# A four-layer graph network on one core: the last group's layer 3 in two parts with a plain product and early statistics, in place of gate products by TensorE and a held TensorE order in the head

## The chip, the cores and the metric

The kernel runs on one core of one Trainium2 chip. The metric is the time of one execution on the device in microseconds (us); the median of several executions is what is compared. The engines are TensorE (PE in the profile; its weight loads are PEld), VectorE (DVE), ScalarE (ACT), GpSimd (POOL) and SyncE (SP), which here only issues transfers. All data is float32.

## The reference, cut to what matters

The input `x` is 128 graphs of 128 nodes by 256 features; `adj` is one 128x128 matrix. Four layers follow one another, each of the form x = x + f(relu(layernorm(x))):

```
# layer 0: gated message passing
in_gate = h @ gate_weight + bias_gate            # one number per node; three such gates
msg_in  = (adj @ h + edge_bias) * sigmoid(in_gate)
msg_out = (adj' @ h + out_edge_bias) * sigmoid(out_gate)
x = x + relu(msg_in + msg_out + h * sigmoid(lp_gate))
# layer 1: causal attention, one head, width 256, adj added to the scores
# layer 2: three graph convolutions, widths 256 -> 512 -> 1024 -> 256, weighting adj*adj
# layer 3:
agg = A_hat @ h                                   # A_hat: normalized adjacency
h1  = relu(batchnorm(agg @ W1.T + b1, g1, be1))   # 256 -> 512
out = batchnorm(h1 @ W2.T + b2, g2, be2)          # 512 -> 256
x   = x + out
```

The two batchnorms of layer 3 take mean and variance per feature over all 128 x 128 rows. Nothing behind the first batchnorm can start before the last graph's product with W1 is known, and nothing behind the second before the last product with W2.

## The kernel before, in words

Graphs are taken in 32 groups of four (G = 4, `NG` = 32, `LAST` = 31); with columns as nodes a group is T = 512 wide.

**First pass** (lines 115 to 851). Layers 0, 1, 2 and the first half of layer 3 run group by group. Each layer is a Python generator (`layer0`, `layer1`, `layer2`, `layer3`) that yields between steps. A string says which generator advances next: `FILL` (line 818) for the head, where group 0 runs in two halves of two graphs (`a`, `c` for layer 0, `b`, `d` for layer 1), `A` is layer 0 of group 1, `p` is `prepare` (weights turned and combined) and `w` stands for 12 idle turns; `TURN` (line 805) for each group; `FINAL` (line 808) for the last one. In `TURN` and `FINAL`, `C` is layer 2 of the group, `D` layer 3 of the group before, `d` layer 3 of this group. The strings set priorities; a scheduler then lays out each engine's queue, and may bring forward what it holds ready. In the head `in_turn` (line 86) holds TensorE's instructions to the order of the string. Instructions given through `keep_in_program_order` keep theirs.

**Products by seven.** `seven` (line 454) computes a product of two 2x2 block matrices with seven half-size products instead of eight: operands are sums of blocks (`sums`, line 406, four VectorE operations; `seven_of`, line 231, for weights), and results are put together through `kept` copies on ScalarE (line 461) and sums on VectorE in `put`. Its accumulators are x, y and z (`pz_x`, `pz_y`, `pz_z` in layer 3), x being used five times.

**Norm** (line 357). For each graph bn_stats and bn_aggr on VectorE give mean and variance; 1/sqrt is a `pow` on GpSimd; ScalarE applies scale, shift and ReLU (line 378). For whole groups the four small steps are on GpSimd (lines 369 to 372); for halves eps and shift are on VectorE (lines 219 and 375) and only `pow` on GpSimd (line 221).

**Layer 0** (line 489). Groups 0 and 1 (`g < 2`): `turn` transposes `h` on TensorE into `h0T`, and three-column products with `gwT` give the gates (line 504). Other groups: twelve scalar_tensor_tensor on VectorE with accumulator (line 513) against `gw`, the gate weights broadcast to all partitions. Then a sigmoid (line 521), and the mixing matrix `cmb` from `ain`, `aout` and `ident` scaled by the gates (lines 530 to 537), with the `eb` copies behind (line 539).

**Layer 3** (line 767). Norm, product with `ahT` into `gT` (`mixed`, `pg`), sums, then `seven` with the turned W1. In `put` ScalarE copies or VectorE sums a quarter into `z`; when both halves of a column pair are in, bn_stats takes 512 columns per feature chunk into `stats1` (line 789) and `z` goes to DRAM, except for the last group, which stays.

**Crossing.** Groups 0 to 29 are aggregated early (`most1`); after the loop `last1` takes groups 30 and 31, TensorE turns `ident` 60 times (`awake(60)`), and `bn_affine` (line 853) joins both into a scale and a shift per feature.

**Second pass** (lines 878 to 1002). Group 31 first, then 0 to 30 (`ORDER`): ReLU with scale and shift on ScalarE (line 939), the product with W2 by `seven` (`po_x`, `po_y`, `po_z`), results `O` kept in SBUF, statistics through `TOLD`/`tell`: for each half of the features one bn_stats of 512 columns, told one step later (line 921). **End:** `last2` takes the last group of the order, `bn_affine` again, then for each group scale and shift on ScalarE (line 1017), transposes on TensorE, the sum with `x` on VectorE (line 1030) and the store. Loads of `x` for this (`x3i`) start during the second pass and go on during the stores.

**Loads in the head.** `adj` on ScalarE's queue, the gate weights once as three rows on GpSimd's queue (for `gwT`), and everything else on SP in the order of the code, `gw` after w3. A dummy sigmoid on one column (line 189) loads the sigmoid table at the start.

Of the kernel before, what the change touches and what calls it, by code (L numbers as in the profile page):

```python
# [22 lines left out]
def kernel(  # L23
# [60 lines left out]
    behind = {}  # L84

    def in_turn(at, engines):

        for i in nc.cur_bb.bb.instructions[at:]:
            if i.engine in engines:
                if i.engine in behind:  # L90
                    tc.add_manual_dep(
                        i, behind[i.engine],
                        mybir.DependencyInfo(
                            mybir.DependencyClass.NoSync, mybir.DependencyReason.DATA
                        ),
                        reason="in_turn",
                    )
                behind[i.engine] = i.name

# [18 lines left out]
    nc.scalar.dma_start(adj_sb, adj)  # L118
# [31 lines left out]
    stats1 = weights.tile([P, FC, NG, 6], FP, name="stats1")  # L150
    stats2 = const.tile([P, DC, NG, 6], FP, name="stats2")

    nc.gpsimd.memset(nhalf, -0.5)
    nc.gpsimd.memset(gb, 0.0)
    w = passA.enter_context(tc.tile_pool(name="work", bufs=2))
# [22 lines left out]

    gwr = bw2t[:3, 0, :]
    gwT = weights.tile([P, DC, 3], FP, name="gwT")  # L180
    for i, v in enumerate((gate_weight, out_gate_weight, loop_gate)):
        nc.gpsimd.dma_start(
            gwr[i : i + 1, :], bass.AP(tensor=v.tensor, offset=v.offset, ap=[[D, 1], [1, D]])
        )
    nc.sync.dma_start(gb[:, 0:1], bias_gate)
    nc.sync.dma_start(gb[:, 1:2], out_bias_gate)

    table = const.tile([P, 1], FP, name="table")
    nc.scalar.activation(table, nhalf[:, 0:1], AF.Sigmoid)

# [13 lines left out]
    for i, v in enumerate((gate_weight, out_gate_weight, loop_gate)):  # L204
        nc.sync.dma_start(
            gw[:, i, :], bass.AP(tensor=v.tensor, offset=v.offset, ap=[[0, P], [1, D]])
        )
# [55 lines left out]
    pw = bank([P, DC, 3], "pgw")  # L263
    for c in range(DC):
        nc.tensor.transpose(pw[:, c, :], gwr[:, c * P : (c + 1) * P], ident[:3, :3])
    nc.vector.tensor_copy(gwT, pw)
# [8 lines left out]
    def prepare():  # L275
# [57 lines left out]
        yield  # L333
        SETS["b"] = seven_of(bw1T, "bw1T")
# [22 lines left out]
    def norm(g, layer, bs=ALL):  # L357
# [8 lines left out]
        rs = small.tile([P, n], FP, tag="rs", name=f"rs{tail}")  # L366
        sh = small.tile([P, n], FP, tag="sh", name=f"sh{tail}")
        if n == G:
            nc.gpsimd.tensor_scalar(rs, mv[:, :, 1], LN_EPS, None, ALU.add)  # L369
            nc.gpsimd.tensor_tensor(rs, rs, nhalf[:, :n], ALU.pow)  # L370
            nc.gpsimd.tensor_scalar(sh, mv[:, :, 0], -1.0, None, ALU.mult)
            nc.gpsimd.tensor_tensor(sh, sh, rs, ALU.mult)  # L372
        else:
            inv_sqrt(rs, mv[:, :, 1], LN_EPS)
            nc.vector.scalar_tensor_tensor(sh, mv[:, :, 0], -1.0, rs, ALU.mult, ALU.mult)
# [10 lines left out]

    def turn(dst, h, bs, name):

        for c in range(DC):
            pt = bank([P, len(bs), P], f"{name}_{c}")  # L390
            for k, b in enumerate(bs):
                nc.tensor.transpose(pt[:, k, :], h[:, b, c * P : (c + 1) * P], ident)
            evict = nc.vector.tensor_copy if c else nc.scalar.copy
            evict(columns(dst, c, bs), pt.rearrange("p b n -> p (b n)"))
# [94 lines left out]
    def layer0(g, bs=ALL):  # L489
# [5 lines left out]
        gate_bias = gb[:, None, :].to_broadcast([P, n, 3])  # L495
        if g < 2:

            hT = tile_of(g, bs, [P, DC, T], "dT", f"h0T_{g}", 2)
            turn(hT, h, bs, f"ph_{tail}")
            yield  # L500
            pl = bank([P, n, 3], f"pl_{tail}")
            for k, b in enumerate(bs):
                for c in range(DC):
                    nc.tensor.matmul(
                        pl[:, k, :], hT[:, c, b * P : (b + 1) * P], gwT[:, c, :],
                        start=(c == 0), stop=(c == DC - 1),
                    )
            nc.vector.tensor_tensor(gl, pl, gate_bias, ALU.add)
        else:
            gs = w.tile([P, D], FP, tag="gs", name=f"gs_{tail}", bufs=1)  # L510
            for k, b in enumerate(bs):
                for i in range(3):
                    nc.vector.scalar_tensor_tensor(  # L513
                        gs, h[:, b, :], 1.0, gw[:, i, :], ALU.mult, ALU.mult,
                        accum_out=gl[:, k, i : i + 1],
                    )
                if k == n // 2 - 1:
                    yield
            nc.vector.tensor_tensor(gl, gl, gate_bias, ALU.add)
# [18 lines left out]
        for k, b in enumerate(bs):  # L538
            nc.scalar.activation(bias[:, b, :], eb, AF.Copy, scale=gt[:, k, 0:1])
# [227 lines left out]
    def layer3(g):  # L767
# [11 lines left out]
        def put(ij, pb, other):  # L779
            i, j = ij  # L780
            dst = z[j][:, :, i * T // 2 : (i + 1) * T // 2]
            if other is None:
                nc.scalar.copy(dst, pb)
            else:
                nc.vector.tensor_tensor(dst, pb, other, ALU.add)
# [285 lines left out]
```

## Time and profile before

Time before: median 2590.16 us of 5 executions, 2589.49 to 2592.59.

| | |
|---|---|
| profiled execution, time | 2592.59 us |
| its span in the trace | 2590.6 us |
| mean granted TensorE clock | 0.993 |
| first layer-2 product of group 0 starts | 72.68 us |
| period of a steady group in the first pass | 70.8 us |
| last layer-3 product of the first pass ends | 2315.67 us |
| first product of the second pass starts | 2322.05 us |
| period of a group in the second pass | 6.04 us |
| last product of the second pass starts | 2517.14 us |
| first scaling for the output starts | 2522.47 us |
| last store issued from | 2579.50 us |

The page of the profile gives busy times and the span in 40 slices. The timeline lists instructions in order of time: start, length, engine, line, operation, output and inputs, shape, count, and in brackets the idle time of the engine before it and what ended that. A float32 matmul shows as two records; a transpose as one. The busy time by windows gives, for a stretch, its length, the busy time of PE, PEld, DVE, ACT and POOL with the number of instructions, the granted clock, the share of the DMA engines and GB/s.

### The profile page before, as it was taken

The numbers are of one execution on the slowest core, as the hardware profiler recorded it, in microseconds if no ns is written. First come the engines' busy times: TensorE is split into PE (matmuls) and PEld (weight loads), VectorE is DVE, ScalarE is ACT, GpSimd is POOL, SyncE is SP. The second block draws the span as 40 slices with busy tenths as digits, with TensorE's granted clock in tenths as the row PEclk, the third lists the DMA queues.
The fourth block names the chain that finished last, engine by engine and source line by source line (L and its number), as shares of the span: only waits on it lengthen the run. The fifth ranks groups of instructions, "written<-read, shape, count | busy, mean of one in ns | idle before, by whom it ended". The sixth has DMA issues, their size and how long they took to land.

```text
span 2590.6 us, 40769 instructions
## 1 busy us (share of the span) xinstructions
PE 2539.6 (98%) x15331; PEld 2295.0 (89%) x15331; DVE 1907.1 (74%) x4788; ACT 1288.6 (50%) x2576; POOL 288.1 (11%) x566
## 2 busy tenths in 40 slices
PE   7999999999999999999999999999999999999995
PEld 5999999999999999999999999999999999888875
DVE  6777777777777777777777777777777776558876
ACT  4554445444444554444444445544454444337766
POOL 1111011111111111011111110111111111000001
PEclk9999999999999999999999999999999999999998
DMA  3000000000000000000000000000000000035559
GB/s 134 15 34 33 33 33 25 25 33 34 33 26 25 33 33 33 33 33 24 26 33 34 33 25 26 33 33 33 34 33 17 34 25 25 25 123 192 176 185 386
DMA packets 49656, 143.07 MB, mean 55 GB/s; under 512 B 4258, under 2 KB 23220, under 8 KB 45492
## 3 DMA queue, kind: packets, MB, share of 16 engines
q1 hardware_dynamic: 42740, 116.81, 12.3%
q0 software_dynamic: 6576, 23.60, 2.6%
q8 instruction: 121, 1.98, 0.3%
q14 instruction: 75, 0.61, 0.1%
q10 hardware_dynamic: 144, 0.07, 0.0%
HBM read 73.48 MB, written 66.98 MB: 54 GB/s over the span
## 4 chain that ended last, share of the span: by engine, by line
PE 94%; DVE 1%; DMA 1%; ACT 1%; POOL 0%; issue 0%; SPq 0%; DVEq 0%; POOLq 0%
PE p_x L446 17%; PE p_x L429 9%; PE p_z L446 8%; PE pmu L401 4%; PE p_z L429 4%; PE pz_x L446 4%; PE p_y L446 4%; PE po_x L951 4%; PE pu_x L429 4%; PE pg L401 2%; PE ps L630 2%; PE pm L555 2%; PE p_y L429 2%; PE pqv_x L587 2%; PE py L660 2%; PE pr L760 2%
## 5 line engine op out<-in xcount | busy, mean ns | idle before, releaser
L378 ACT ACTIVATE h<-x,sh,rs 128x256 f32<-128x256 f32 x512 | 268.8, 589 | 356.8 <-POOL sh L372 346.1
L446 PE MATMUL p_x<-uT,w 128*128 128x256 f32 x1024 | 242.2, 379 | 0.0
L732 ACT ACTIVATE h2T<-h2T 128x512 f32<-128x512 f32 x192 | 120.6, 628 | 229.8 <-DVE h2T L731 229.8
L446 PEld LDWEIGHTS p_x<-uT,w 128*128 128x128 f32 x1024 | 189.7, 190 | 23.2
L363 DVE BATCH_NORM_STATS2 st<-x 128x6 f32<-128x256 f32 x512 | 191.0, 414 | 2.2
L369 POOL TENSOR_SCALAR rs<-mv 128x4 f32<-128x4 f32 x125 | 29.8, 239 | 1351.6 <-ACT h2T L732 1061.0
L513 DVE SCALAR_TENSOR_TENSOR gs<-h,gw 128x256 f32<-128x256 f32 x360 | 150.3, 418 | 27.6 <-ACT h L378 22.4
L461 ACT COPY p_t<-p_x 128x512 f32<-128x512 f32 (+1 forms) x192 | 96.6, 503 | 109.7 <-PE p_x L446 102.8
L370 POOL TENSOR_TENSOR rs<-rs,nhalf 128x4 f32<-128x4 f32 x125 | 145.0, 1160 | 0.0
L401 PEld LDWEIGHTS pmu<-a2T,u 128*128 128x128 f32 x1024 | 119.3, 192 | 14.8 <-issue 14.8
L429 PEld LDWEIGHTS p_x<-w,h2T 128*128 128x128 f32 x1024 | 124.3, 192 | 3.3
L685 ACT ACTIVATE u<-u 128x512 f32<-128x512 f32 x93 | 58.6, 631 | 133.7 <-DVE u L684 133.7
L429 PE MATMUL p_x<-w,h2T 128*128 128x128 f32 x1024 | 124.6, 275 | 0.0
L446 PE MATMUL p_x<-us,w_s 128*128 128x256 f32 x512 | 121.2, 379 | 0.0
L446 PE MATMUL p_x<-uT,w_s 128*128 128x256 f32 x512 | 121.1, 379 | 0.0
L446 PE MATMUL p_y<-uT,w 128*128 128x256 f32 x512 | 121.0, 379 | 0.0
L446 PE MATMUL p_z<-us,w_s 128*128 128x256 f32 x512 | 121.0, 379 | 0.0
L446 PE MATMUL p_z<-us,w 128*128 128x256 f32 x512 | 121.0, 379 | 0.0
L401 PE MATMUL pmu<-a2T,u 128*128 128x128 f32 x1024 | 119.5, 275 | 0.0
L761 DVE TENSOR_TENSOR x<-pr,x 128x512 f32<-128x512 f32 x64 | 43.7, 682 | 90.4 <-PE pr L760 90.4
L446 PEld LDWEIGHTS p_z<-us,w_s 128*128 128x128 f32 x512 | 97.3, 190 | 13.2
L446 PEld LDWEIGHTS p_z<-us,w 128*128 128x128 f32 x512 | 97.3, 190 | 13.2
(317 smaller groups left out, 6174.1 us busy)
## 6 DMA issues: line engine op xcount, KB each, us to landing
z<-zo SPq DMA_DIRECT2D x62, 512.0 KB, 2.6
zi<-z SPq DMA_DIRECT2D x31, 1024.0 KB, 4.8
x<-x POOLq DMA_DIRECT2D x32, 512.0 KB, 3.4
x<-in_x_dram SPq DMA_DIRECT2D x31, 512.0 KB, 4.0
out_dram<-x3i SPq DMA_DIRECT2D x30, 512.0 KB, 12.8
x3i<-x SPq DMA_DIRECT2D x19, 512.0 KB, 5.2
x3i<-x POOLq DMA_DIRECT2D x13, 512.0 KB, 10.1
w<-in_L_gnn_W_dram SPq DMA_DIRECT2D x1, 2048.0 KB
```

The source lines that it names most:

```text
L363: nc.vector.bn_stats(st[:, k, :], xt[:, b, :])
L370: nc.gpsimd.tensor_tensor(rs, rs, nhalf[:, :n], ALU.pow)
L378: nc.scalar.activation(h[:, b, :], xt[:, b, :], AF.Relu, bias=sh[:, k : k + 1], scale=rs[:, k : k + 1])
L401: nc.tensor.matmul(pm[:, k, :], src[:, b, c * P : (c + 1) * P], aT, start=True, stop=True)
L429: nc.tensor.matmul(pb[:, rr, :], a_r[r][:, c, rr * P : (rr + 1) * P], b_r[r][:, c, :wide], start=(first and rr == 0 and c == 0), stop=(c = ...
L446: nc.tensor.matmul(pb[:, jj, :], b_r[r][:, c, at : at + P], a_r[r][:, c, :], start=(first and jj == 0 and c == 0), stop=(c == nk - 1), ski ...
L461: nc.scalar.copy(t, pb)
L513: nc.vector.scalar_tensor_tensor(gs, h[:, b, :], 1.0, gw[:, i, :], ALU.mult, ALU.mult, accum_out=gl[:, k, i : i + 1],)
L555: nc.tensor.matmul(pm[:, r, :], cmbT[:, b, :], h[:, b, :], start=True, stop=True)
L685: nc.scalar.activation(dst, dst, AF.Relu)
L732: nc.scalar.activation(dst, dst, AF.Relu)
L951: nc.tensor.matmul(pb, BW2R[r][:, c, :], a_r[r][:, c, :], start=(first and c == 0), stop=(c == FC // 2 - 1), skip_group_check=True,)
```

## The change: what it does

In the head: the gates of groups 0 and 1 are computed as in all other groups, on VectorE; `turn`, `gwT` and its loads and turns, the dummy sigmoid and `in_turn` go; `FILL` is another string; half norms take the four GpSimd steps of whole norms; `adj` is loaded by SP ahead of `x`, and `gw` and the two gate biases by ScalarE's queue at the start; the `eb` copy of each graph is given ahead of its `ain` copy. In layer 3: groups 30 and 31 give their statistics by halves of 256 columns, from PSUM and ahead of the copy where ScalarE copies; group 31 takes its norm and its product with `ahT` in two halves and multiplies with W1 plainly, by quarters (i, j), without `sums` and `seven`; a copy `bw1T_12` keeps the block of W1 that `seven_of` overwrites. `FINAL` is another string, `awake(60)` becomes `awake(44)`. `bn_affine` has its steps in another order and two fewer after `pow`. In the second pass the last group's statistics are taken by halves in the same way.

```diff
-    nc.scalar.dma_start(adj_sb, adj)
+    nc.sync.dma_start(adj_sb, adj)
...
+    stats1 = weights.tile([P, FC, NG + 2, 6], FP, name="stats1")
+    stats2 = const.tile([P, DC, NG + 1, 6], FP, name="stats2")
+    bw1T_12 = weights.tile([P, F1 // 2], FP, name="bw1T_12")
...
+    for i, v in enumerate((gate_weight, out_gate_weight, loop_gate)):
+        nc.scalar.dma_start(
+            gw[:, i, :], bass.AP(tensor=v.tensor, offset=v.offset, ap=[[0, P], [1, D]])
+        )
+    nc.scalar.dma_start(gb[:, 0:1], bias_gate)
+    nc.scalar.dma_start(gb[:, 1:2], out_bias_gate)
...
-    table = const.tile([P, 1], FP, name="table")
-    nc.scalar.activation(table, nhalf[:, 0:1], AF.Sigmoid)
...
         yield
+        nc.scalar.copy(bw1T_12, bw1T[:, 0, F1 // 2 :])
         SETS["b"] = seven_of(bw1T, "bw1T")
...
+        nc.gpsimd.tensor_scalar(rs, mv[:, :, 1], LN_EPS, None, ALU.add)
+        nc.gpsimd.tensor_tensor(rs, rs, nhalf[:, :n], ALU.pow)
         sh = small.tile([P, n], FP, tag="sh", name=f"sh{tail}")
-        if n == G:
...
-            inv_sqrt(rs, mv[:, :, 1], LN_EPS)
-            nc.vector.scalar_tensor_tensor(sh, mv[:, :, 0], -1.0, rs, ALU.mult, ALU.mult)
+        nc.gpsimd.tensor_scalar(sh, mv[:, :, 0], -1.0, None, ALU.mult)
+        nc.gpsimd.tensor_tensor(sh, sh, rs, ALU.mult)
...
-        if g < 2:
-
-            hT = tile_of(g, bs, [P, DC, T], "dT", f"h0T_{g}", 2)
-            turn(hT, h, bs, f"ph_{tail}")
...
         for k, b in enumerate(bs):
+            nc.scalar.activation(bias[:, b, :], eb, AF.Copy, scale=gt[:, k, 0:1])
             nc.scalar.activation(cmb[:, b, :], ain, AF.Copy, scale=gt[:, k, 0:1])
...
-        for k, b in enumerate(bs):
-            nc.scalar.activation(bias[:, b, :], eb, AF.Copy, scale=gt[:, k, 0:1])
...
+        parts = [ALL] if g < LAST else HALVES
+        for bs in parts:
+            h = norm(g, 3, bs)
+            yield
+        gT = tile_of(g, parts[0], [P, DC, T], "dT", f"gT_{g}", 2)
+        for i, bs in enumerate(parts):
+            mixed(gT, h, ahT, f"pg_{g}_{i}", (nc.vector.tensor_copy,), bs)
+            if g < LAST:
+                ex = w.tile([P, 3, 1, T // 2], FP, tag="ex", name=f"gs_{g}", bufs=2)
+                gs = sums(nc.vector, quarters_t(gT), ex)
+            yield
...
+            if other is not None:
+                nc.vector.tensor_tensor(dst, pb, other, ALU.add)
+            if g >= LAST - 1:
+                at = 2 * g - LAST + 1 + i
+                for jj in range(2):
+                    nc.vector.bn_stats(
+                        stats1[:, 2 * j + jj, at, :], (pb if other is None else dst)[:, jj, :]
+                    )
             if other is None:
                 nc.scalar.copy(dst, pb)
...
+        if g < LAST:
+            yield from seven(columns_by_half(gs, SETS["b"], 0), put, [P, 2, T // 2], f"pz_{g}")
+            return
+        for i, j in (0, 0), (1, 0), (0, 1), (1, 1):
+            pb = bank([P, 2, T // 2], f"pz_{g}_{i}_{j}")
+            for jj in range(2):
+                for c in range(DC):
+                    at = (2 * j + jj) * P
+                    b = bw1T_12[:, jj * P : (jj + 1) * P] if (c, j) == (0, 1) else bw1T[:, c, at : at + P]
+                    nc.tensor.matmul(
+                        pb[:, jj, :], b, gT[:, c, i * T // 2 : (i + 1) * T // 2],
+                        start=(jj == 0 and c == 0), stop=(c == DC - 1), skip_group_check=True,
+                    )
+            put((i, j), pb, None)
+            yield
...
-    FINAL = "CCCCCCCCCCCCCCCCCCDCCDCCDdDDdDddDdDdddd"
+    FINAL = "CCCCCCCCCCCCCCCCCCDCCCCDDdDDddDdDdDdddd"
...
-    FILL = "aacaaccacapcabpccpbdbdAdbdAdddbAbbAdwbAbAAdpppbdp"
+    FILL = "acpacaacacaccabpcpbdbddAddbAddbbbAdwAbAbAAdpAbpdpp"
...
-        in_turn(at, KEPT)
...
-    awake(60)
+    awake(44)
...
+        d, e, sc, sh = (const.tile([P, nch], FP, name=f"{k}_{name}") for k in ("d", "e", "sc", "sh"))
+        nc.vector.tensor_scalar(var, var, 1.0 - share, BN_EPS, ALU.mult, ALU.add)
         nc.vector.tensor_tensor(d, mean1, mean, ALU.subtract)
+        nc.vector.scalar_tensor_tensor(var, var1, share, var, ALU.mult, ALU.add)
+        nc.vector.scalar_tensor_tensor(e, d, share * (1.0 - share), d, ALU.mult, ALU.mult)
+        nc.vector.tensor_tensor(var, var, e, ALU.add)
+        inv_sqrt(sc, var, 0.0)
         nc.vector.scalar_tensor_tensor(mean, d, share, mean, ALU.mult, ALU.add)
         nc.vector.tensor_tensor(mean, mean, bias, ALU.add)
+        nc.vector.tensor_tensor(d, bias, mean, ALU.subtract)
         nc.vector.tensor_tensor(sc, sc, gam, ALU.mult)
+        nc.vector.tensor_tensor(sh, d, sc, ALU.mult)
+        nc.vector.tensor_tensor(sh, sh, bet, ALU.add)
...
+            last = g == ORDER[-1]
+            told = stats2[:, j, LAST + i, :]
             if other is None:
+                if last:
+                    tc.keep_in_program_order(nc.vector.bn_stats(told, pb))
                 nc.scalar.copy(dst, pb)
             else:
                 in_order(dst, pb, other, ALU.add)
+                if last:
+                    TOLD.append((told, dst))
```

## Prediction

> **What bounds the kernel now.** I read the page first: the busy shares, then the span in 40 slices.
>
> ```profile
> PE 2539.6 (98%) x15331; PEld 2295.0 (89%) x15331; DVE 1907.1 (74%) x4788; ACT 1288.6 (50%) x2576; POOL 288.1 (11%) x566
> ...
> PE   7999999999999999999999999999999999999995
> ...
> PEclk9999999999999999999999999999999999999998
> DMA  3000000000000000000000000000000000035559
> ```
>
> TensorE is busy in every slice but the first and the last, at full granted clock. The list of waits has no long TensorE wait between 75 us and 2299 us, so an edit counts only in three places: the head (0 to 73 us, until the first layer-2 product of group 0 at 72.68 us), the crossing from the first pass to the second (2299 to 2322 us), and the end (from 2517 us). The busy time by windows shows the head:
>
> ```profile
> 10.00:20.00 10.00, 6.88 (x26) 5.75 (x27) 5.87 (x21) 4.04 (x13) 0.00 (x0) 1.00 1.05 386
> 20.00:30.00 10.00, 8.01 (x37) 6.66 (x35) 8.53 (x17) 4.54 (x12) 1.62 (x1) 0.98 0.78 256
> ...
> 50.00:60.00 10.00, 9.12 (x41) 6.37 (x41) 7.30 (x28) 5.69 (x15) 1.39 (x2) 0.83 0.00 0
> ```
>
> Columns are PE, PEld, DVE, ACT and POOL busy, clock, DMA share, GB/s. No engine is full: the head is a chain through all of them, with VectorE at 48.4 us of the first 70 (the seven windows' DVE column added). The timeline shows the crossing:
>
> ```profile
> 2299.25 1.03 PE L446 MATMUL pz_y<-gT,bw1T 128*128 128x256 f32 x4
> ...
> 2304.88 1.21 PE L401 MATMUL pg<-ahT,h 128*128 128x128 f32 x8 [1.45 <-ACT h L378]
> ...
> 2314.54 1.13 PE L446 MATMUL pz_x<-gT,bw1T_s 128*128 128x256 f32 x4 [0.79 <-DVE zo L785]
> ...
> 2315.50 6.71 PE L108 MATMUL awake<-ident 128*128 128x128 f32 x60
> 2315.70 0.58 ACT L783 COPY zo<-pz_x 128x512 f32<-128x512 f32 x1 [3.19 <-PE pz_x L446]
> ...
> 2316.32 1.28 DVE L789 BATCH_NORM_STATS2 stats<-zo 128x6 f32<-128x512 f32 x2 [0.28 <-ACT zo L783]
> ...
> 2319.19 1.01 POOL L221 TENSOR_TENSOR sc_bn<-sc_bn,nhalf 128x4 f32<-128x4 f32 x1 [15.00 <-DVE sc_bn L219]
> ...
> 2322.05 1.30 PE L951 MATMUL po_x<-zo,bw2T 128*128 128x256 f32 x4
> ```
>
> Here TensorE waits for the last group's norm, ends its last product at 2315.67 and then only turns `ident` until the statistics have gone through copy, bn_stats, affine and ReLU: 6.38 us. In the end stage the transfers are full:
>
> ```profile
> 2580.00:2585.00 5.00, 0.00 (x0) 0.00 (x0) 0.00 (x0) 0.00 (x0) 0.00 (x0) 0.50 1.02 419
> ```
>
> The DMA share is 0.97 to 1.03 in every window from 2520 to 2585 us.
>
> **Crossing, TensorE.** After `pr` ends (about 2299.3) before still has six products of group 30 (pz_y to the last pz_x; one starts every 0.865 us), `pg` (1.79) and seven products of group 31: 5.19 + 1.79 + 6.05 = 13.03 us; they take until 2315.67, 16.4 us, so 3.3 us are stalls. After: FINAL gives `pr` ahead of pz_x, 0.86 us earlier, and seven products remain (6.05), `pg` (1.79) and the plain product: 16 matmuls of 256 columns, 32 records of 0.216 us, 6.92. From 2298.4 that is 14.76, so 2313.2 if dense. Halves shorten what stalls: a two-column `pow` is 0.70 where four are 1.03, two `h` 1.09 where four are 2.07, and the four sums on `gT` (0.42 each) go. I leave 0.9 us of the stalls: 2314.1, a gain of 1.6. Bounds: 2.5 (no stall left) and -0.8 (all 3.3 stay).
>
> **Crossing, statistics to first product.** From TensorE's end: two 256-column bn_stats from PSUM. No row has one; VectorE's copy of 128x256 out of PSUM (L394) is 0.42, its 128x256 sum from SBUF 0.42, and bn_stats of that size 0.42 with 0.34 to the next, so 0.76, with 1.28 (the 512 form) as the other end. Then 0.28 of aggregation, d, e and the sum in steps of 0.20 (0.66 with the hand-over), `pow` 1.01, three steps for sc and sh (0.66) and 0.9 to the ReLU's product: 4.3 us. The 44 turns (60 take 6.55, so 0.109 each) last 4.8 and start 0.17 before that end; the product stands behind them, so 4.65. Gain 6.38 - 4.65 = 1.7 (0.9 to 2.0). The copies of `z` on ScalarE lie beside the statistics. The second pass's loads are issued at 2314.54, held by the last `zo` sum (L785) of group 31, an instruction that the change drops; I cost that at nothing, and at +1 us if bw2T (0.5 MB behind 1 MB) should land last. Extra bn_stats on VectorE, 16 of 0.42 for 8 of 0.68, are 1.3 us more, against 1.7 + 2.1 less for the four sums on `gT` and three sums into `zo`.
>
> **End.** The last group's halves put two more bn_stats (0.42) between VectorE's sums in 2514 to 2517, which TensorE's last product waits for (0.52): up to +0.8. Shorter statistics and affine give 1.2 back to ScalarE, but full DMA queues hide it: what starts them is the last product. I take +0.3 (-0.6 to +0.8). So the crossing and end give 1.6 + 1.7 - 0.3 = **3.0 us**.
>
> **Head, what goes and comes.** TensorE loses 16 turns and 32 gate records: by their rows 1.28 + 1.09 + 1.04 and 1.84 + 0.59 + 1.44 + 1.85, about 9.1 us of TensorE time, which was not the bound. VectorE gets 24 gate sums; steady groups show their pace:
>
> ```profile
> 78.11 0.42 DVE L513 SCALAR_TENSOR_TENSOR gs<-h,gw 128x256 f32<-128x256 f32 x1
> 78.45 0.08 DVE L513 DVE_READ_ACCUMULATOR gs<-h,gw 128x1 f32 x1
> 78.57 0.42 DVE L513 SCALAR_TENSOR_TENSOR gs<-h,gw 128x256 f32<-128x256 f32 x1
> ```
>
> 24 x 0.46 = 11.0; h0T copies (1.5), gwT (0.15) and six norms' eps and shift (1.9) go: **+7.4 us** on VectorE. Its idle time in 0 to 70 is 21.6, of which 3.7 lie before adj_sb lands and 3.8 in one wait for w1, so 14 can take it, but not for nothing. Steps on the chain:
> - x is issued behind adj on SP: +0.45 (one issue). SP loses the three gw and two gb issues, ScalarE's queue gets five in its idle first 3 us.
> - Six half norms on GpSimd alone: the four-column form takes 1.83 (2302.37 to 2304.20), less 0.33 for two columns is 1.5, against 1.2 now (54.07 to 55.28); three lie on a half's chain: +0.8.
> - Group 0's gates: six sums 2.8 against 3.5 now (turn at 8.71 to products' end at 12.2): -0.7.
> - The `eb` copy now stands ahead of each `ain` copy on ScalarE (rows 0.45 each), so both are through two `eb` later, and `cmb` with them: +0.9. In later groups ScalarE, half idle, hides that.
> - Group 1's twelve sums fall at 40 to 60 us, among the softmax and norm-2 steps. About ten VectorE steps of the chain each wait half a gate sum: 10 x 0.23 = +2.3.
> - The order on TensorE is no longer held: group 0's second `pc` waits today from 19.5 (its cmb done) to 26.1 behind Wqkv's turns. Free, it gains between 0 and 6.6; VectorE is 85% busy there, so nearer the low end: -1.0.
> - One sigmoid table load (1.28) comes back; it fits between `h` (about 10.3) and the gate sums' end (about 11.3 or later): 0 to +1.3, I take 0.
>
> Sum: 0.45 + 0.8 - 0.7 + 0.9 + 2.3 - 1.0 = **+2.8 us**; the ends are -2.8 (the order gives all 6.6) and +10.9 (7.4 of VectorE's time, x, norms, `eb` and the load exposed).
>
> The Trainium skill, "ScalarE: Activation LUTs", What ACT_TABLE_LOAD costs, speaks against this last edit: a switch costs a drain besides the load, 2.66 us in all. Here the dummy's ACTIVATE starts at 2.50, straight after the load (1.21 + 1.28); an estimate by the page makes the head 1.4 us worse where the row adds nothing.
>
> **Sum.** -3.0 + 2.8 = -0.2 us: the profiled execution's 2592.59 (span 2590.6 and 2.0 around it) would be 2592.4. That execution was the slowest of five; from the median 2590.16 I get **2590.0**: no change, since a measurement of this kernel tells about 0.2%, 5.2 us.
>
> **Rivals.**
> - *VectorE becomes the head's bound.* For it: 85% in 20 to 30 us and 73% in 50 to 60, chains crossing it at every step, and scheduling that already lets a weight sum wait 3.8 us in front of the gates. Against: 14 us of idle time. All 7.4 + 0.45 + 0.8 + 0.9 exposed, less 3.0: +6.6, **2596.7**, slower. It is slower than before from the point where the head loses over 3.0 us. Chance 0.15.
> - *The freed order wins the head.* The second half comes 6 us sooner instead of 1: head 2.8 - 5.3 = -2.5, all -5.5, **2584.7**. For it the 6.6 us above; against it that the two halves meet at the same VectorE. Chance 0.10.
> - *The crossing does not get shorter*: the half norms arrive no sooner or the second pass's loads hold the first product. Only 0.5 of the 3.3 comes: 2.8 - 0.5 + 0.3 = +2.6, **2592.8**. For it: `pg` still needs x of the last `pr`. Chance 0.12.
> - *Forecast*, 2586.5 to 2593.5: 0.63.
>
> A second rule: idle TensorE loses its clock. Between 2518.3 and 2523.3 it idles 5 us here and its granted clock is then 0.63 over 6.7 us, so if the 44 turns fall short by much, the crossing pays some 2.5 us. The skill's "TensorE: Matmul & The Clock Gate", Part 1, puts the limit at an idle window of about 3.4 us; the shortfall of the third rival, 6.2 - 4.8 = 1.4 us, would by that cost no clock.
>
> **How the numbers follow.** The range goes about half into the first two rivals, 2584.8 to 2596.5, and leaves out about 0.13. Faster by over 0.2% (under 2585.0): half of the second rival and a little, 0.06. Slower (over 2595.3): most of the first and a little, 0.14. Within: 0.80.
>
> **What would show it.** The first p_x of group 0 at 73 to 76 us (72.68 now) confirms the head; 80 or more the first rival; under 71 the second. From the first matmul of the last `pr` (2297.53 now) to the end of the last pz product are 18.1 us now and should be 17.4, with the first po_x 4.65 us behind it instead of 6.4. The final stage should keep its DMA share of 1.0 and its length. A long TensorE wait between 75 and 2299 us, or a second pass whose groups no longer take 6.04 us, would make the prediction wrong.

## The result, and the profile after

The changed kernel takes 2597.24 us (median of 24 executions, 2595.32 to 2599.85), the kernel before 2591.35 (44 executions, 2589.38 to 2593.55): ratio 1.0023, 95% interval 1.0017 to 1.0028, so 5.9 us slower. The forecast was 2590.0, no change, with a range from 2584.8 to 2596.5; the measured time lies above it. It is that of the first rival (2596.7); whether it came about by that rival's mechanism is a question for runs.

The profiled execution of the changed kernel took 2595.68 us (span 2593.6), 3.1 more than that of before. That is less than the 5.9 of the medians: the one of before lay 1.2 above its median, this one 1.6 below.

The page's first lines, read as those of before:

```profile
PE 2530.4 (98%) x15269; PEld 2287.4 (88%) x15269; DVE 1912.2 (74%) x4823; ACT 1291.1 (50%) x2576; POOL 287.9 (11%) x585
...
PE   5999999999999999999999999999999999999995
```

TensorE's first slice (65 us) falls from 7 to 5, and no other does. The head again by windows (PE, PEld, DVE, ACT, POOL busy, clock, DMA share, GB/s), and the end:

```profile
10.00:20.00 10.00, 7.15 (x28) 6.13 (x28) 6.72 (x35) 7.86 (x20) 1.21 (x4) 1.00 1.05 390
20.00:30.00 10.00, 5.11 (x12) 2.73 (x12) 9.56 (x26) 1.78 (x6) 0.00 (x0) 0.61 0.86 280
50.00:60.00 10.00, 6.69 (x29) 4.83 (x30) 8.35 (x33) 8.15 (x20) 1.55 (x4) 0.83 0.00 0
2580.00:2585.00 5.00, 0.00 (x0) 0.00 (x0) 0.00 (x0) 0.00 (x0) 0.00 (x0) 0.50 1.02 419
```

From 20 to 30 us TensorE has 12 matmul records where it had 37, and VectorE is busy 9.56 of 10 us instead of 8.53. That looks like a bound by VectorE; the runs below speak against it. The last window is as before. The crossing in the timeline:

```profile
2304.50 1.12 PE L710 MATMUL pr<-s,a2T 128*128 128x512 f32 x2 [0.46 <-ACT s L696]
2305.46 1.03 PE L407 MATMUL pz_x<-gT,bw1T 128*128 128x256 f32 x4
...
2311.40 0.94 PE L362 MATMUL pg<-ahT,h 128*128 128x128 f32 x6 [0.34 <-ACT h L348]
...
2320.80 4.97 PE L92 MATMUL awake<-ident 128*128 128x128 f32 x44
...
2321.01 0.76 DVE L742 BATCH_NORM_STATS2 stats<-pz 128x6 f32<-128x256 f32 x2 [0.96 <-PE pz L764]
...
2322.74 1.01 POOL L198 TENSOR_TENSOR sc_bn<-mv_most,nhalf 128x4 f32<-128x4 f32 x1 [13.00 <-DVE mv_most L839]
...
2325.61 1.10 PE L919 MATMUL po_x<-zo,bw2T 128*128 128x256 f32 x4
```

The last statistics now come 0.05 us behind TensorE's last product (2320.96), read from PSUM, and the first po_x follows 4.65 us behind it instead of 6.38. How much later than in the kernel before each point comes:

| point | before | after | later by |
|---|---|---|---|
| first p_x of group 0 | 72.68 | 78.64 | 5.96 |
| end of the last layer-3 product | 2315.67 | 2320.96 | 5.29 |
| first po_x | 2322.05 | 2325.61 | 3.56 |
| first scaling for the output | 2522.47 | 2524.95 | 2.48 |
| last store issued | 2579.50 | 2582.56 | 3.06 |

The first of these points, in the kernel before and in the changed kernel:

```profile
72.68 1.99 PE L446 MATMUL p_x<-uT,w 128*128 128x256 f32 x8
```

```profile
78.64 1.99 PE L407 MATMUL p_x<-uT,w 128*128 128x256 f32 x8
```

In this pair the head loses 6 us and the tail wins back about 3. The first p_x lies between the 73 to 76 us that would have confirmed my head and the 80 of the first rival. Between 80 and 2296 us TensorE waits once, 0.8 us (0.5 in the kernel before), so next to nothing else was lost on the way.

### The profile page after: what moved, and what is told of

It reads as the page before. It is cut to its first block, busy times and chain, and to the rows that moved or that the text cites. A ratio compares the mean times of both kernels' runs of the same rounds, so it can differ in the third digit from the quotient of the medians.

```text
span 2593.6 us, 40693 instructions
## 1 busy us (share of the span) xinstructions
PE 2530.4 (98%) x15269; PEld 2287.4 (88%) x15269; DVE 1912.2 (74%) x4823; ACT 1291.1 (50%) x2576; POOL 287.9 (11%) x585
## 4 chain that ended last, share of the span: by engine, by line
PE 94%; DMA 2%; DVE 2%; ACT 1%; POOL 1%; issue 0%; ACTq 0%; DVEq 0%; SPq 0%; POOLq 0%
PE p_x L407 17%; PE p_x L390 9%; PE p_z L407 8%; PE pmu L362 4%; PE p_z L390 4%; PE p_y L407 4%; PE pu_x L390 4%; PE po_x L919 4%; PE pz_x L407 4%; PE pg L362 2%; PE ps L580 2%; PE pm L362 2%; PE pm L500 2%; PE p_y L390 2%; PE pr L710 2%; PE pqv_x L537 2%
## 5 line engine op out<-in xcount | busy, mean ns | idle before, releaser
L341 POOL TENSOR_SCALAR rs<-mv 128x4 f32<-128x4 f32 (+1 forms) x132 | 31.3, 237 | 1432.8 <-ACT h2T L682 1027.3
L459 DVE SCALAR_TENSOR_TENSOR gs<-h,gw 128x256 f32<-128x256 f32 x384 | 160.5, 418 | 33.3 <-ACT h L348 27.4
L342 POOL TENSOR_TENSOR rs<-rs,nhalf 128x4 f32<-128x4 f32 (+1 forms) x132 | 148.8, 1127 | 0.0
```

The costliest lines, as they stand in the source:

```text
L459: nc.vector.scalar_tensor_tensor(gs, h[:, b, :], 1.0, gw[:, i, :], ALU.mult, ALU.mult, accum_out=gl[:, k, i : i + 1],)
```

## Experiments

My first theory (A) was that the tail does what I forecast and the head loses by VectorE's 24 gate sums; its rivals were GpSimd's norm steps (N), the loads (L), the string (S), the table loads (D) and the order on TensorE.

Each run is timed against the kernel before on the same chip (median of some 20 to 30 executions, 2591.0 to 2592.0). "Ratio" is to the kernel before; 0.001 is 2.6 us, and an interval reaches about 0.0009 to each side, so two runs of mine that differ by less than some 2.5 us are not told apart by the medians alone.

### The two halves of the change

`tail_only` has layer 3, the crossing, the second pass and the end of the changed kernel, and all of the old head; `head_only` the opposite.

> The kernel before with the tail of the change alone: layer 3 of the last group in two parts with the plain product, early statistics, FINAL, 44 turns, the new affine and the halves of the second pass's last group. Theory A (the tail gains what the traces show from TensorE's last layer-3 product to the second pass, 1.0 + 1.7, and the head alone is at fault): 2.4 to 3.2 us faster than before. Rival B (the traced pair of executions is 3.1 us apart and the medians 5.9, so a part of the tail's gain is taken back behind the crossing): within 1 us of before.

> The change's head with the tail of the kernel before. Theory A: the first p_x of group 0 at 78 to 79 us in its trace and a median 6 us (the trace's difference) to 8.8 us (5.9 plus the tail's gain) slower than before. Rival B: 5.5 to 6 us slower, the same as the whole change.

Measured: the tail alone 2587.85 us, ratio 0.9987 (0.9979 to 0.9996), 3.3 us faster; the head alone 2599.55, ratio 1.0032 (1.0020 to 1.0043), 8.4 us slower (5.2 to 11.1). The tail's forecast of 3.0 holds. The head's 2.8 does not.

### Parts taken out of the changed kernel

Held order again: `in_turn` after every letter of the new FILL. Sigmoid behind: group 1's sigmoid is bound to come after group 0's exponentials.

```diff
+        in_turn(at, KEPT)
```

```diff
+        if g == 1:
+            tc.add_manual_dep(
+                nc.cur_bb.bb.instructions[-1], exps[-1],
...
```

> The changed kernel with TensorE's instructions in the head held to the order of FILL, as before did it, and nothing else. If the freed order is what costs (the scheduler puts the second half's scores behind the first half's transposes), it is 2 us or more faster than the changed kernel. If the order was not the cause, it is within 1 us of it; if freeing it helped, as I took with 1 us, it is slower by 1 us or more.

> The changed kernel with group 1's sigmoid held behind all four exponentials of group 0, so that the tables are switched once and not three times between 46 and 54 us. Theory C (the two added loads of 1.28 us lie on the chain): 1.5 to 2.6 us faster than the changed kernel, first p_x at 76 to 77 us. Rival D (VectorE is what the chain waits for there, the loads lie beside its work): within 0.5 us of it.

Measured: held 2599.44, ratio 1.0030 (1.0019 to 1.0041); sigmoid behind 2597.86, ratio 1.0027 (1.0017 to 1.0037). Against before, holding the order adds 2.4 us to the loss of the changed kernel; that is within the intervals, so freeing the order did no harm that shows and may have helped. Table switches among the exponentials cost nothing that shows.

Next, half norms with eps and shift on VectorE as before; adj on ScalarE's queue and gw on SP behind x; the dummy sigmoid; and, in the kernel before, the gates of both groups on VectorE with gw loaded behind adj on ScalarE's queue.

```diff
-    nc.sync.dma_start(adj_sb, adj)
+    nc.scalar.dma_start(adj_sb, adj)
...
-        nc.scalar.dma_start(
+        nc.sync.dma_start(
             gw[:, i, :], bass.AP(tensor=v.tensor, offset=v.offset, ap=[[0, P], [1, D]])
```

> The changed kernel with the half norms as before the change: eps, the shift and its scaling on VectorE, only pow on GpSimd. Theory N (the four GpSimd steps of each half norm, of which rows show 1.05 to 1.32 us in place of 0.23 while VectorE works on wide tiles, are most of the head's loss): 3 to 5 us faster than the changed kernel, ratio to the kernel before 0.9995 to 1.0012, first p_x of group 0 near 74 to 76 us. Theory A (VectorE's 24 gate sums are the loss, VectorE being nearly full): handing VectorE 12 more small steps gains nothing or costs up to 1.5 us, ratio 1.002 to 1.003, p_x at 78 to 80.

> The changed kernel with the loads of the head's start back in their queues: adj on ScalarE's queue, gw and the gate biases on SP behind the two halves of x. x lands 1.5 us later in the changed kernel than before it (5.70 against 4.20), my prediction had 0.45. Theory L (a late start passes down the whole head): 1 to 2.5 us faster than the changed kernel, ratio to the kernel before 1.0013 to 1.0020. Theory A (what comes behind is VectorE's queue, which absorbs an early start): within 0.5 us of the changed kernel, ratio 1.0020 to 1.0026.

> The changed kernel with the dummy sigmoid at the start, so that the first gates find the table loaded. If the load of 1.28 us fits beside the gate sums, as I predicted: within 0.4 us of the changed kernel, ratio to the kernel before 1.0020 to 1.0026. If it is exposed: 1.3 us faster, ratio about 1.0018; by the skill's price of 2.66 us for a switch, ratio about 1.0013.

> The kernel before with one part of the head's change alone: the gates of groups 0 and 1 by VectorE's sums, without the turns, gwT and the products on TensorE; gw is loaded on ScalarE's queue where gwT's rows were; the string, the held order, the norms, the dummy sigmoid and all of the tail stay. Theory A (VectorE's 24 sums are the loss): 5 to 8 us slower than the kernel before, ratio 1.0019 to 1.0031, first p_x of group 0 at 78 to 81. Theory N or L (the sums cost what I predicted, 2.3 less 0.7, and the rest comes from norms, loads and eb): 0.5 to 2.5 us slower, ratio 1.0002 to 1.0010, p_x at 73.5 to 75.5.

Measured: norms 2598.02, ratio 1.0028 (1.0017 to 1.0039); x first 2595.20, 1.0015 (1.0006 to 1.0023); dummy sigmoid 2596.76, 1.0020 (1.0011 to 1.0029); gates alone 2595.49, 1.0017 (1.0008 to 1.0026), 4.5 us slower than before. So the gates, with their early gw, cost something by themselves, and the norms are not the loss (theory N falls). The loads put back give back 1.7 us, which is not told apart from nothing.

### Sizing single terms

```diff
-        if g < 2:
+        if g < 1:
```

is `before_dve1`, group 1's gates alone on VectorE. `after_string` has the old FILL (49 letters, as the new one has; the diff above prints one A too many in the new one); `before_free` drops the call of `in_turn`; `after_eb` puts the `eb` copies behind the `ain` copies again.

> The kernel before with the gates of group 1 alone on VectorE: twelve sums among group 0's softmax, no h0T copies and no products for this group; group 0 keeps its gates on TensorE and all loads stay where they were. It sizes one term of my head sum, +2.3. Theory A1 (group 1's sums push group 0's softmax back; in the kernel with both groups on VectorE, 4.5 us slower than before, the last exponential ends at 49.0 us and the second py starts at 55.1, where before had 46.1 and 50.2): 3 to 4.5 us slower than the kernel before, ratio 1.0012 to 1.0018, second py at 53 to 55. Theory A0 (group 0's own sums and the earlier load of gw are the loss): within 1 us, ratio 0.9998 to 1.0004. My forecast's term: 2.3 slower, ratio 1.0009.

> The changed kernel with FILL of the kernel before; it has the same letters, each as often, in another sequence. Theory S (the new string lets group 1's gate sums and sigmoid in between the exponentials of group 0's two halves: in the changed kernel the second half's first exponential starts at 54.2 us behind two more table loads, in the kernel before at 45.2): 2 to 4 us faster than the changed kernel, ratio to the kernel before 1.0007 to 1.0015, and the second half's exponentials ahead of group 1's sigmoid. Theory A (VectorE's load is the loss, in whatever sequence): within 1 us of the changed kernel, ratio 1.0018 to 1.0027.

> The kernel before without in_turn: TensorE's instructions in the head are laid out by the scheduler. My term was -1.0 of at most -6.6: the second pc no longer waits from 19.5 to 26.3 us behind the turns of Wqkv. If it holds here too: 0.5 to 2.5 us faster than the kernel before, ratio 0.9990 to 0.9998, second pc ahead of wqkvT. The rival: with gates on TensorE the held order is what keeps turns of weights behind the chain, and freeing it lets them in front: 1 to 4 us slower, ratio 1.0004 to 1.0015.

> The changed kernel with the eb copies behind the ain copies again, as before the change. My term was +0.9 for their new place. If it holds: 0.5 to 1.5 us faster than the changed kernel, ratio to the kernel before 1.0017 to 1.0021. If ScalarE has room for them where they are: within 0.4 us, ratio 1.0021 to 1.0025.

Measured: group 1's gates 2593.43, ratio 1.0008 (0.9999 to 1.0017), 1.9 us; old string 2597.02, 1.0022 (1.0013 to 1.0031); free order in the old head 2591.17, 0.9999 (0.9990 to 1.0008); `eb` 2597.71, 1.0024 (1.0014 to 1.0033). Group 1's term agrees with my forecast of 2.3, though the interval holds 0 as well. String, order (in the old head) and `eb` are nothing that can be measured. In the run with the old string all four exponentials stand together again and the granted clock from 20 to 30 us is 1.00 instead of 0.61, yet the time is the same, so the split softmax is not the cause. Nor is the clock of that stretch by itself; but from 50 to 70 us this run has lower clocks than the changed kernel (0.55 and 0.77 against 0.83 and 1.00), so it doesn't clear the clock of the whole head.

### Is VectorE the bound?

`after_late` and `tail_late` hold W2's four sums (1.2 us each), which nothing needs before layer 2, behind the second half's layer-1 norm (their letter `p` moves in FILL as well); `before_load` gives VectorE twelve more sums that nobody reads; `before_x` moves the loads alone.

```diff
         SETS["2"] = seven_of(w2, "w2")
+        tc.add_manual_dep(
+            nc.cur_bb.bb.instructions[-4], NORMED[1, G // 2],
...
```

```diff
+            if g == 0:
...
+                        nc.vector.scalar_tensor_tensor(
+                            gs, h[:, b, :], 1.0, h[:, b, :], ALU.mult, ALU.mult,
+                            accum_out=unused[:, k, i : i + 1],
+                        )
```

```diff
-    nc.scalar.dma_start(adj_sb, adj)
+    nc.sync.dma_start(adj_sb, adj)
...
+        nc.scalar.dma_start(
+            gw[:, i, :], bass.AP(tensor=v.tensor, offset=v.offset, ap=[[0, P], [1, D]])
+        )
+    nc.scalar.dma_start(gb[:, 0:1], bias_gate)
+    nc.scalar.dma_start(gb[:, 1:2], out_bias_gate)
```

> The changed kernel with W2's four VectorE sums (128x1024, 1.2 us each, 4.8 in all) held behind the statistics of the second half's layer-1 norm; in the changed kernel they stand at 21.8 to 32.3 us between steps of the chain. Nothing needs them before layer 2 of group 0. Theory V (VectorE is the bound until the first layer-1 norm: from 4 us to that norm's h it is busy 23.4 of 29.2 us here and 18.6 of 25.0 in the kernel before, idle about 6 in both, so its work counts one to one): that h comes 3 to 5 us sooner and the time is 2 to 4.5 us below the changed kernel, ratio to the kernel before 1.0005 to 1.0015. Theory L (late x and the chain's own latency are the loss): within 1 us of the changed kernel, ratio 1.0018 to 1.0027.

> The tail's part of the change alone, as in the kernel that has it with the head of before, and in that head W2's four VectorE sums held behind the second half's layer-1 norm. Theory V: VectorE bounds the old head's first 30 us too, so 1.5 to 4 us faster than the tail alone, ratio to the kernel before 0.9972 to 0.9982, which would be the fastest of all. Theory L: the old head is a chain with room on VectorE, so within 0.8 us of the tail alone, ratio 0.9984 to 0.9991.

> The kernel before with the changed kernel's loads alone: adj on SP ahead of x, gw and the two gate biases on ScalarE's queue at the start; gates stay on TensorE for groups 0 and 1. x lands about 1.5 us later (4.2 to 5.7) where my term was +0.45. Theory L: 1.2 to 2.5 us slower than the kernel before, ratio 1.0005 to 1.0010. Theory V: VectorE's wait of 3.8 us for w1 in this head swallows a later x, so within 0.7 us, unless w1 lands later as well, then as much slower as w1 is late.

> The kernel before with twelve more sums on VectorE in group 0's layer 0, of the form of the gate sums (0.46 us each, 5.5 in all), whose results nobody reads; the gates themselves stay on TensorE and no load moves. Theory V: those of the first half fill VectorE's wait for w1, the rest counts: 2 to 4 us slower than the kernel before, ratio 1.0008 to 1.0015. Theory L: VectorE has room, within 0.8 us, ratio 0.9997 to 1.0003.

Measured: `after_late` 2597.57, ratio 1.0021 (1.0012 to 1.0030); `tail_late` 2587.45, 0.9983 (0.9974 to 0.9992), the fastest median, not told apart from the tail alone; `before_x` 2597.06, 1.0021 (1.0012 to 1.0030), 5.5 us slower than before; `before_load` 2590.73, 0.9996 (0.9987 to 1.0005). Theory V, that VectorE bounds the first 30 us, falls: 5.5 us more work on VectorE cost nothing in the old head, and 4.8 us less in the stretch where it is fullest brought nothing in either. The windows of `before_load` show that the work was done:

```profile
10.00:20.00 10.00, 7.75 (x29) 6.49 (x30) 7.44 (x33) 3.78 (x12) 0.55 (x1) 1.00 1.05 385
20.00:30.00 10.00, 7.72 (x34) 6.34 (x32) 8.35 (x17) 4.57 (x12) 0.71 (x1) 1.00 0.76 250
```

VectorE has 12 instructions more from 10 to 20 us (33 against 21) and 1.57 us more of busy time; the twelve sums start between 8.55 and 17.99 us. The first p_x comes at 71.65. The loads alone, with all gates on TensorE, cost almost as much as the whole change. What they do, in the timeline of `before_x`:

```profile
0.72 0.41 ACTq L156 DMA_DIRECT2D gw<-n_L_gnn_gate_weight_dram  x1
0.73 0.39 SPq L118 DMA_DIRECT2D adj_sb<-in_adj_dram  x1
...
1.17 0.93 SPq L129 DMA_DIRECT2D x<-in_x_dram  x2
...
4.58 0.37 SPq L199 DMA_DIRECT2D wide<-in_L_gnn_Wqkv_dram  x1
...
6.09 0.75 DVE L363 BATCH_NORM_STATS2 st<-x 128x6 f32<-128x256 f32 x2 [1.43 <-DMA x<-in_x_dram]
```

and in the list of SP's waits (us in total, times, longest):

```profile
SPq L199 <- DMA gw<-n_L_gnn_gate_weight_dram: 2.5, 1, 2.5
```

x's first statistics start at 6.09 us where before has 4.20, and SP, which issued Wqkv at 2.70, does so at 4.58: from 2.1 to 4.58 it issues nothing. The delay of 1.9 us grows to 2.8 at the first gates and 4.0 at the first `h` of layer 1 (table below), and further, in the same run, at 38 to 44 us:

```profile
38.48 0.69 DVE L239 TENSOR_TENSOR w_s<-w 128x512 f32<-128x512 f32 x1
...
40.84 1.52 POOL L372 TENSOR_TENSOR sh<-sh,rs 128x4 f32<-128x4 f32 x1
41.01 0.69 DVE L242 TENSOR_TENSOR w<-w 128x512 f32<-128x512 f32 x1
41.61 0.69 DVE L241 TENSOR_TENSOR w_s<-w,w_s 128x512 f32<-128x512 f32 x1
42.40 1.09 ACT L378 ACTIVATE h<-x,sh,rs 128x256 f32<-128x256 f32 x2 [3.64 <-POOL sh L372]
43.39 0.35 ACT L394 COPY hT<-pt 128x256 f32<-128x256 f32 x1
...
43.79 2.07 PE L606 MATMUL pqv<-hT,m_qk 128*128 128x256 f32 x4 [4.44 <-ACT hT L394]
```

One GpSimd step of group 1's norm now falls under a row of VectorE sums and takes 1.52 us (0.20 in the kernel before, at 37.09). Group 1's `h` waits for it on ScalarE, the copy `hT` of group 0's second half stands behind that `h` in ScalarE's queue, and TensorE idles 4.44 us for the copy.

### Which load, and is it so in the changed kernel?

`before_adj` is the kernel before with adj on SP ahead of x, one word. `after_rows` takes gw's 384 KB from the changed kernel: three rows of 1 KB on ScalarE's queue behind adj, spread by TensorE.

```diff
+    for i, k in (0, 2), (2, 1):
+        pg = bank([P, k, D], f"pgw_{i}")
+        nc.tensor.matmul(
+            pg.rearrange("p a d -> p (a d)"), ones, gwr[:, i : i + k, :].rearrange("p a d -> p (a d)"),
+            start=True, stop=True,
+        )
+        nc.scalar.copy(gw[:, i : i + k, :], pg)
```

> The kernel before with adj loaded by SP ahead of x and nothing else changed: gw stays on SP behind w3. This is my term of +0.45 as I put it. Theory G (gw's 384 KB beside x and the weights are what the loads cost): x lands 0.3 to 0.7 us later, the time within 1 us of the kernel before, ratio 0.9997 to 1.0004. Theory Q (SP's queue is the cost: whatever stands ahead of x and the weights on it passes down the head): 3 to 6 us slower, ratio 1.0012 to 1.0023.

> The changed kernel with gw not loaded in 128 copies of each row: three rows of 1 KB come in on ScalarE's queue behind adj (which goes back there), and TensorE spreads them over the partitions by a product with a row of ones, two PSUM banks that ScalarE copies to gw. All other parts of the changed head stay, the VectorE gates of both groups too. Theory G: x lands at 4.2 to 4.6 us, the first weights 1 to 2 us sooner, and 3 to 5.5 us of the changed kernel's loss come back: ratio to the kernel before 1.0002 to 1.0012. Theory of the gates (VectorE's sums are the loss, the loads only in the head of before): within 1.5 us of the changed kernel, ratio 1.0017 to 1.0027.

Measured: `before_adj` 2591.83, ratio 1.0002 (0.9993 to 1.0011), x 0.13 us later; `after_rows` 2597.59, 1.0022 (1.0013 to 1.0030). In the old head theory G holds: adj ahead of x is free, so what is left as the cost is gw (with the two gate biases) early on ScalarE's queue. In the changed kernel, taking gw's bytes away brings nothing, although x is there 1.3 us sooner. Where that went, in the timeline of `after_rows`:

```profile
9.12 1.09 ACT L357 ACTIVATE h<-x,sh,rs 128x256 f32<-128x256 f32 x2 [3.49 <-POOL sh L354]
...
10.12 0.56 ACT L248 COPY gw<-pgw 128x512 f32<-128x512 f32 x1
...
10.72 0.42 DVE L468 SCALAR_TENSOR_TENSOR gs<-h,gw 128x256 f32<-128x256 f32 x1 [2.36 <-ACT gw L248]
...
13.59 0.42 DVE L218 TENSOR_TENSOR w_s<-w 128x256 f32<-128x256 f32 x1 [2.44 <-DMA w<-in_L_gnn_W_dram]
...
17.28 0.16 DVE L474 TENSOR_TENSOR gl<-gl,gb 128x6 f32<-128x6 f32 x1
```

`h` is 1.26 us sooner, but the copy of gw stands behind two `h` on ScalarE, and then W1's sum waits 2.44 us for its load with all but one of the first half's gate sums behind it on VectorE. The first gates are ready at 17.28; in the changed kernel at 17.36. This run therefore exchanges one wait for another, and does not show that the gates alone are the loss.

The same pattern, one stretch later, in `after_late`, whose first layer-1 `h` comes 4.1 us sooner (29.21 against 33.34):

```profile
57.74 2.50 PE L92 MATMUL awake<-ident 128*128 128x128 f32 x12
60.07 1.06 PE L370 MATMUL pm<-a2T,h 128*128 128x128 f32 x8
63.67 0.48 PE L500 MATMUL pc<-ident,m 128*128 128x128 f32 x1 [2.54 <-DVE m L490]
63.94 1.92 PE L653 MATMUL pu<-w,mT 128*128 128x512 f32 x2
```

`pu`, layer 2's first product of group 0, stands behind group 1's `pc` on TensorE, which waits 2.54 us for mixing matrices that wait for group 1's gates. It starts at 63.94; in the changed kernel at 64.27. Points of the head in one table:

| us | before | loads alone | gates alone | after | after_late | after_rows | after_xfirst |
|---|---|---|---|---|---|---|---|
| first statistics of x | 4.20 | 6.09 | 4.06 | 5.70 | 6.25 | 4.38 | 4.20 |
| first `h` | 7.94 | 10.05 | 7.97 | 10.38 | 10.90 | 9.12 | 8.85 |
| gates, first half | 14.71 | 17.54 | 12.54 | 17.36 | 17.98 | 17.28 | 13.38 |
| first `h` of layer 1 | 29.16 | 33.19 | 30.91 | 33.34 | 29.21 | 33.43 | 32.49 |
| first exponential | 44.35 | 50.94 | 47.25 | 49.95 | 45.65 | 50.87 | 48.27 |
| first `pu` | 58.28 | 63.95 | 62.92 | 64.27 | 63.94 | 65.68 | 64.03 |
| first p_x | 72.68 | 78.35 | 77.20 | 78.64 | 79.90 | 80.06 | 78.41 |

These are single executions; the same head differed from one to the next (p_x at 72.68 in the kernel before, 70.18 in the tail alone).

The last column, the changed kernel with gw and adj put back, is a second test of the loads there. x is on time (4.20) and the first gates come 4.0 us sooner than in the changed kernel, yet `pu` and p_x come only 0.2 sooner: the lead is gone by then. From 40 to 50 us VectorE, which the sums of group 1's gates now share with group 0's softmax, is busy 9.41 of 10 us in this run (6.67 in the kernel before):

```profile
40.00:50.00 10.00, 7.05 (x46) 6.04 (x46) 9.41 (x36) 5.98 (x12) 0.00 (x0) 0.97 0.01 2
```

The first and the last of these twelve sums, and group 1's gates behind them:

```profile
41.53 0.41 DVE L459 SCALAR_TENSOR_TENSOR gs<-h,gw 128x256 f32<-128x256 f32 x1
...
50.05 0.42 DVE L459 SCALAR_TENSOR_TENSOR gs<-h,gw 128x256 f32<-128x256 f32 x1
...
51.39 0.16 DVE L465 TENSOR_TENSOR gl<-gl,gb 128x12 f32<-128x12 f32 x1
...
51.59 0.21 ACT L467 ACTIVATE gt<-gl 128x12 f32<-128x12 f32 x1 [1.13 <-DVE gl L465]
```

Followed back from the first p_x, this run's chain of work goes through all twelve. So a bound by VectorE in this later stretch, which neither `before_load` nor `after_late` tests, is not excluded.

## Why the prediction was wrong

**Crossing and end: right.** Statistics to first product: 1.7 forecast, 6.38 - 4.65 = 1.73 measured, each piece near its row; the product stood behind the 44 turns, as forecast. TensorE: 1.6 forecast, about 1.06 measured (FINAL's p_y 6.35 later, the last product's end 5.29). The stalls after `pr` were as left: 15.50 us for 14.76 dense, 0.74 against my 0.9. But `pr` ended 0.7 later than I had put it, 0.46 of it a wait of its second part for ScalarE. My check, 18.1 to 17.4 us from `pr` to the end, was framed wrongly: the first part of `pr` now starts at 2301.23, ahead of a whole product of layer 2 (`p_x`, 1.95) that my count left out, and the stretch is now 19.7. The end did not cost 0.3 but gave about 0.5 (3.56 to 3.06), of 1.1 us that the scaling came sooner. That full queues hid the rest fits the DMA share of 1.00 to 1.03 from 2530 us on in both kernels, but no run tests it. The tail as a whole: 3.0 forecast, 3.3 (1.0 to 5.4) measured.

**The step that failed: "x is issued behind adj on SP: +0.45 (one issue). SP loses the three gw and two gb issues, ScalarE's queue gets five in its idle first 3 us."** I counted the issues of the moved loads and not what they carry. The issue behind adj costs nothing measurable (`before_adj`); gw's 384 KB beside x and ahead of the weights, which this sentence booked at nothing, make the loads alone, in the old head, 5.5 us slower (3.1 to 7.8), against 0.45. With it failed the sum it stands in: +2.8 for the head, 8.4 (5.2 to 11.1) measured. In the changed kernel this term is not the whole of that: with the loads put back its loss is 1.7 us less, without gw's bytes 0.3 less, neither told apart from nothing. The wait of 2.4 to 2.5 us on SP stands in both kernels with these loads:

```profile
SPq L176 <- DMA gw<-n_L_gnn_gate_weight_dram: 2.4, 1, 2.4
```

(the changed kernel; Wqkv is issued at 4.51). I had the line for this: `gw` stood behind w3 on SP, and the DMA share of 1.05 from 10 to 20 us said that the DMA engines were full from there on.

**Group 0's gates: "-0.7", probably also wrong.** Both groups' gates alone cost 4.5, group 1's alone 1.9; the difference, 2.6, is group 0's, with gw early in it. Each of the two is known to some 2.3 us only, so the times alone don't settle the sign; the trace shows what went against me. The first half's gates do come sooner (12.54 instead of 14.71), but W1's sum waits 3.05 us for its load between them and the mixing steps, and the second half's gates come at 20.67 instead of 17.12. I had seen that wait in the kernel before and had not asked what would stand behind it.

**Group 1's gates: +2.3 forecast, 1.9 (-0.3 to 4.4) measured in the old head.** Right within what can be told.

**Small terms.** `eb` +0.9: put back, no change (0.2 the other way). Norms +0.8: put back, 1.1 us slower, within the interval, so no sign of a cost. Free order -1.0: 2.4 us in the changed kernel, within the interval, and none in the old head. Table load 0: the dummy sigmoid put back gives less than 1 us, not told apart from 0; in the timeline the load stands at 15.95 to 17.23, ahead of the step at 17.36 that completes the gates, so it is hidden. The second exponentials start at 54.20, 0.01 us after a load of 1.28 from 52.91: the 2.66 us that the Trainium skill, "ScalarE: Activation LUTs", What ACT_TABLE_LOAD costs, gives for a switch is not seen here, by 1.38.

**The rival that had the number.** "VectorE becomes the head's bound" gave 2596.7, 0.5 from the result. Up to 30 us the runs speak against its mechanism: work added on VectorE is free, work taken away brings nothing. 9.56 of 10 us busy was no proof of a bound, because W2's sums in it were fill that nothing waited for. From 40 to 52 us its mechanism is not excluded (`after_xfirst`), so whether the number came by it or by luck is open.

**The form of the sum.** Loads alone cost 5.5 and gates alone 4.5 (both hold an early gw), the whole head 8.4; yet no part taken out of the changed kernel gave back more than about 2. So what a part costs alone is not what it gives back. My reading, from single traces: paths through the two halves and group 1 end close to one another, and a part taken away leaves the next one (`after_late`: 4.1 us ahead at layer 1, 0.3 at `pu`; `after_xfirst`: 4.0 ahead at the gates, 0.2 at `pu`). I had added terms along one path.

**Open.** How the 8.4 splits between loads and gates in the changed kernel: no run put the gates back on TensorE there, with or without the loads. How much of it is a lower clock (0.61 and 0.53 from 20 to 40 us, 0.98 and 0.68 in the kernel before): no run tests it. Why SP issues nothing for 2.4 us while gw is under way.

## What to carry to other kernels

Price a load that is moved to the front by its bytes and by what lands behind it, not by its issue: look at what the first compute waits for and at the issue times of the queue beside it. In a start-up phase run each part alone and take each part out alone; if the two answers differ, paths of nearly equal length may meet there, and a sum of terms along one of them is no forecast. Here the tail's part alone, with the old head (2587.85 us, or 2587.45 with W2's sums held back), beats both kernels by 3 to 4 us against before and 9 to 10 against after.

## What the runs showed of the hardware

A GpSimd step of 128x2 to 128x4 elements other than `pow`, 0.19 to 0.24 us by itself, takes up to 1.72 beside VectorE's sums of two SBUF operands (1.05 to 1.72 where they are 512 or 1024 columns wide), and in the rows looked at ends 0.05 to 0.09 us after such a sum. In the changed kernel, VectorE's rows and then GpSimd's:

```profile
29.95 1.19 DVE L218 TENSOR_TENSOR w_s<-w,w_s 128x1024 f32<-128x1024 f32 x1
31.06 1.22 DVE L219 TENSOR_TENSOR w<-w 128x1024 f32<-128x1024 f32 x1
```

```profile
30.12 1.10 POOL L341 TENSOR_SCALAR rs<-mv 128x2 f32<-128x2 f32 x1 [17.81 <-DVE mv L339]
31.30 1.05 POOL L344 TENSOR_SCALAR sh<-mv 128x2 f32<-128x2 f32 x1
```

The sums end at 31.14 and 32.28, the steps at 31.22 and 32.35. The Trainium skill, "SBUF — State Buffer", SBUF: two separate sides, calls the pair of ports that both engines share an exclusive lock for a whole instruction; these rows agree. I had priced the four steps at 1.5 us from a place where VectorE was idle; here they take 3.2 (30.12 to 33.30).
